# A fused interaction network on one core: first block of x in two half tables, transfers reordered, dummy products in TensorE's waits

## The chip, the cores and the metric

The kernel runs on one core of a Trainium2 chip. The metric is device microseconds of one execution, the median of several runs. Before the change it is 750.26 us (three runs, 749.74 to 750.42). The engines are called PE (TensorE, matrix products), DVE (VectorE), ACT (ScalarE), POOL (GpSimd) and SP (SyncE). ACT, SP and POOL also issue transfers, and all transfers share the core's 16 DMA engines.

## The reference

x has 1024 samples of 39 fields with 64 numbers each. Three layers each multiply the fields of the last layer with those of x in every pair and mix the products by a weight matrix; the sums over the 64 numbers are joined and multiplied by fc_w.

```python
def _cin_layer(Xk, X0, W, b):
    O = W.shape[0]
    Hk, Fdim = (Xk.shape[1], X0.shape[1])
    Wr = W.reshape(O, Hk, Fdim)
    return jnp.einsum('bhe,bfe,ohf->boe', Xk, X0, Wr) + b[None, :, None]
X0 = sparse_embedding
Xk = X0
outs = []
for W, b in ((W0, b0), (W1, b1), (W2, b2)):
    Xk = _cin_layer(Xk, X0, W, b)
    outs.append(Xk.sum(axis=-1))
cin_output = jnp.concatenate(outs, axis=-1)
return cin_output @ fc_w.T + fc_b
```

## The kernel before

Only a weighted sum over the third layer's outputs is needed, so the kernel folds W2 with fc_w into a matrix v2 (v in the profile), and v2 with W1 into a matrix T. W0 and T, transposed, lie in the upper and lower 64 rows of a tile called both. From it DVE and ACT pick the weights (pairs) of each product of two fields; PE transposes them (tr), ACT copies them to wa, and then PE multiplies products of fields (p) by wa and adds them up in po.

x is used in 32 blocks of 32 samples, 2048 columns each. A block of x is first copied within DRAM to a table xd whose rows are fields, with one more row of ones; each table holds two blocks. POOL then gathers rows of the table by lists of indices into r (four tiles for a block), u and v (one pair for two blocks). DVE multiplies two gathered tiles into a p.

```python
    xd = [dram.tile([2 * FT, BLK], F32, name=f"xd{k}") for k in range(NTAB)]

    def load(n, engine=nc.sync):
        first = n % 2 * FT
        engine.dma_start(
            xd[n // 2 % NTAB][first : first + F].rearrange("f (b e) -> f b e", e=E),
            xv[:, n * BB : (n + 1) * BB, :],
        )

    def gather_rows(dst, n, k, cols=slice(0, BLK)):
        table = xd[n // 2 % NTAB][: FT if k < 4 else 2 * FT]
        nc.gpsimd.indirect_dma_start(
            dst[:, cols], None, table,
            bass.IndirectOffsetOnAxis(ap=lists[:, k : k + 1], axis=0),
            element_offset=cols.start,
        )
# ... cut: roll gathers the four r tiles of a block, roll_half gathers u and v
        nc.sync.dma_start(fcrow, fc_w)
        nc.scalar.dma_start(w2s, w2.rearrange("o (s n) -> (o s) n", s=2))
        load(0)
        load_ones(0, nc.scalar)
        for s, n in enumerate((NW, F - NW)):
            nc.scalar.dma_start(w0s[H * s : H * s + F, 0 : n * H], w0v[:, s * NW * H : (s * NW + n) * H])
        for s, engine in enumerate((nc.sync, nc.scalar)):
            engine.dma_start(w1s[H * s : H * s + H], w1[:, s * (FH // 2) : (s + 1) * (FH // 2)])
# ... cut
        nc.scalar.copy(warm, warm)          # ACT loads its table of functions here
        for k in range(1, NTAB):
            load_ones(k, nc.sync)
# ... cut
        def spin(n=1):                      # dummy products, whose result nobody reads
            for _ in range(n):
                nc.tensor.matmul(idle[:, 0 : MM // 2], zeros[:, 0:128], zeros, start=True, stop=True)
# ... cut: the index lists
        halves = [slice(0, SUB), slice(SUB, BLK)]
        for cols in halves:
            roll(0, (0, 1, 2), cols)
        load(1, nc.gpsimd)
        roll(0, (3,))
# ... cut: W2 times fc_w gives pv, then v2; W0 is transposed to pw; lists for u and v
        roll_half(0)
        roll(1)
# ... cut: the biases
        load(2, nc.gpsimd)
        load(3, nc.gpsimd)
        copies = (nc.vector.tensor_copy, nc.scalar.copy)
# ... cut: untwine copies transposed fields from PSUM to both, with the engine given
        for s, (a, n) in enumerate(((0, NW), (NW, F - NW))):
            untwine(copies[s], 0, a, n, 1, pw[s], F)
        # ... v2 times W1: 2 products into pv (fields 32 to 38), 4 into pt (fields 0 to 31)
        # ... pv is copied to rest, pt to part, half by DVE and half by ACT
        turn_fields(pt[0], rest, slice(0, FT), NR)
        untwine(copies[0], 1, 2 * NA, NR, 1, pt[0], FT)
        for k in range(2):
            turn_fields(pw[k], part, slice(H * k, H * k + FT), NA)
        for k in range(2):
            untwine(copies[k], 1, NA * k, NA, NA // 2, pw[k], FT)
        spin(2)
```

Then comes the main part. The products of the first three steps are made in halves, PE starts with the first quarter of the first product, and DVE works four steps ahead of PE. A step is one pair of tiles of one block: six steps with r for each block, and one step with u and v for two blocks, the seventh of the first.

```python
    for k, (n, c) in enumerate(steps[:3]):
        p[n, c] = first[k]
        weight_rows(c)
        if not k:
            weight_turn(c)
            spin()
            for m in range(2):
                product(n, c, slice(m * MM, (m + 1) * MM), p[n, c])
        else:
            product(n, c, halves[0], p[n, c])
# ... cut: second halves, fourth product, and the main loop
```

Of the kernel before, what the change touches and what calls it, by code (L numbers as in the profile page):

```python
# [54 lines left out]
F32 = mybir.dt.float32  # L55
# [5 lines left out]
B, F, E, H = 1024, 39, 64, 64  # L61
FH = F * H
# [13 lines left out]
SUB = 1024  # L76
BLK = 2048
NA = 16
NR = F - 2 * NA
NW = 20  # L80
BB = BLK // E
SB = SUB // E
NBLK = B // BB
FT = F + 1
NTAB = 3
# [13 lines left out]
def cin_kernel(ctx: ExitStack, tc: tile.TileContext, x, w0t, b0, w1, b1, w2, b2, fc_w, fc_b, out):  # L99
    nc = tc.nc  # L100
# [4 lines left out]
    dram = ctx.enter_context(tc.tile_pool(name="dram", bufs=1, space=DRAM))  # L105
# [3 lines left out]

    xv = x.rearrange("b f e -> f b e")  # L110
    xd = [dram.tile([2 * FT, BLK], F32, name=f"xd{k}") for k in range(NTAB)]

    def bank(name):
        return psum.tile([128, MM], F32, name=name, tag="po")
# [5 lines that stand above are left out]
            xv[:, n * BB : (n + 1) * BB, :],  # L120
        )

    def gather_rows(dst, n, k, cols=slice(0, BLK)):
        table = xd[n // 2 % NTAB][: FT if k < 4 else 2 * FT]
        nc.gpsimd.indirect_dma_start(  # L125
            dst[:, cols],
            None,
            table,
            bass.IndirectOffsetOnAxis(ap=lists[:, k : k + 1], axis=0),
            element_offset=cols.start,  # L130
        )

    def roll(n, tiles=range(4), cols=slice(0, BLK)):
        for i in tiles:
            gather_rows(rt[n % 2][:, i], n, n % 2 * 4 + i, cols)

    def roll_half(n):
        gather_rows(ut[n // 2 % 2], n, 8)
        gather_rows(vt[n // 2 % 2], n, 9)

    wa = const.tile([128, NCHUNK, 2 * H], F32, name="wa")
    fc = const.tile([H, 3], F32, name="fc")
# [8 lines left out]
    lists = const.tile([128, 10], I32, name="lists")  # L151
    rt = [const.tile([128, 4, BLK], F32, name=f"r{k}") for k in range(2)]
    ut = [const.tile([128, BLK], F32, name=f"u{k}") for k in range(2)]
    vt = [const.tile([128, BLK], F32, name=f"v{k}") for k in range(2)]
# [17 lines left out]
    with prep as prep:  # L172
        w2s = prep.tile([128, FH // 2], F32, name="w2s")
        w1s = prep.tile([128, FH // 2], F32, name="w1s")
        w0s = prep.tile([128, NW * H], F32, name="w0s")
        part = prep.tile([128, NA, H], F32, name="part")
# [4 lines left out]
        ones = prep.tile([16, 2, 128], F32, name="ones")  # L181
# [7 lines left out]

        nc.vector.memset(zeros, 0.0)  # L193
        nc.vector.memset(ones, 1.0)
        nc.vector.memset(fc2, 0.0)
        nc.vector.memset(v2, 0.0)
        nc.vector.memset(warm, 0.0)

        def load_ones(k, engine):
            engine.dma_start(xd[k][F::FT].rearrange("r (p c) -> p r c", c=128), ones)  # L200

        w0v = w0t.rearrange("b a h -> b (a h)")
        nc.sync.dma_start(fcrow, fc_w)  # L203
        nc.scalar.dma_start(w2s, w2.rearrange("o (s n) -> (o s) n", s=2))
        load(0)
        load_ones(0, nc.scalar)
        for s, n in enumerate((NW, F - NW)):
            nc.scalar.dma_start(w0s[H * s : H * s + F, 0 : n * H], w0v[:, s * NW * H : (s * NW + n) * H])
        for s, engine in enumerate((nc.sync, nc.scalar)):
            engine.dma_start(w1s[H * s : H * s + H], w1[:, s * (FH // 2) : (s + 1) * (FH // 2)])  # L210
        nc.gpsimd.iota(place, pattern=[[0, 1]], base=0, channel_multiplier=1)
        for i in range(3):
            for k, by in enumerate((STEP[i + 1], BASE[i + 1], EXTRA[i + 1] - K)):
# [3 lines left out]
        bothv = both.rearrange("p (a b) -> p a b", b=FT)  # L217
        nc.gpsimd.memset(bothv[0:H, :, F], 0.0)
        nc.scalar.copy(warm, warm)
        for k in range(1, NTAB):  # L220
            load_ones(k, nc.sync)


        pv = [bank("pv") for _ in range(2)]
        pt = [bank("pt") for _ in range(2)]
        idle = bank("idle")
        pw = [bank("pw") for _ in range(2)]
# [3 lines left out]
        def spin(n=1):  # L231
            for _ in range(n):
                nc.tensor.matmul(idle[:, 0 : MM // 2], zeros[:, 0:128], zeros, start=True, stop=True)  # L233
# [45 lines left out]
        for s in range(2):  # L279
            nc.gpsimd.tensor_copy(fcrow2[:, :, s], fcrow[:, 2 * H : 3 * H])  # L280

        halves = [slice(0, SUB), slice(SUB, BLK)]
        for cols in halves:
            roll(0, (0, 1, 2), cols)
        load(1, nc.gpsimd)
        roll(0, (3,))


        one = ones[0:1, 0, 0:1]
# [36 lines left out]
        for s in range(2):  # L326
            for k in range(NW // 2):
                n = min(128, (F - NW * s) * H - k * 128)
# [20 lines left out]
        nc.vector.tensor_scalar(half, half, float(FT), None, ALU.mult)  # L349
        nc.vector.tensor_scalar(lists[:, 8:10], fields_of[:, 4:6], half, None, ALU.add)  # L350
        roll_half(0)
        roll(1)
        for k, t in enumerate((b1, b2)):
            nc.gpsimd.dma_start(bias[:, k : k + 1], t.rearrange("(h o) -> h o", o=1))
# [7 lines left out]
        copies = (nc.vector.tensor_copy, nc.scalar.copy)  # L362

        def untwine(copy, half, a, n, by, src, width):


            for s in range(2):
                m = (n + 1 - s) // 2
                at = a + s * by
                step = 2 if by == 1 else 1  # L370
                copy(  # L371
                    bothv[H * half : H * half + H, at : at + step * (m - 1) + 1 : step, 0:width],
                    src[H * s : H * s + H, 0 : m * FT].rearrange("p (a b) -> p a b", b=FT)[
                        :, :, 0:width
                    ],
                )

        for s, (a, n) in enumerate(((0, NW), (NW, F - NW))):
            untwine(copies[s], 0, a, n, 1, pw[s], F)
        w1v = w1s.rearrange("o (h f) -> o f h", f=F)  # L380
        for s in range(2):
            rows = slice(H * s, H * s + H)
# [23 lines left out]
        def turn_fields(to, src, rows, n):  # L406
            for a in range(0, n, 2):
                m = min(2, n - a)
                nc.tensor.transpose(  # L409
                    to[0 : m * H, a // 2 * FT : a // 2 * FT + FT],  # L410
                    src[rows, a : a + m, :].rearrange("b a h -> b (a h)"),
                    unit[rows, rows],
                )

        turn_fields(pt[0], rest, slice(0, FT), NR)
        untwine(copies[0], 1, 2 * NA, NR, 1, pt[0], FT)
        for k in range(2):
            turn_fields(pw[k], part, slice(H * k, H * k + FT), NA)
        for k in range(2):
            untwine(copies[k], 1, NA * k, NA, NA // 2, pw[k], FT)  # L420
        spin(2)
        first = [prods.tile([128, BLK], F32, name="p", tag="p") for _ in range(3)]


# [128 lines left out]
    p = {}  # L553
# [14 lines left out]
    n, c = steps[3]  # L568
# [98 lines left out]
```

## Time and profile before

| engine | busy us | share of the span |
|---|---|---|
| PE | 740.6 | 99% |
| DVE | 643.9 | 86% |
| POOL | 324.4 | 43% |
| ACT | 163.8 | 22% |

The profiled execution has a span of 750.1 us. PE is busy nearly all of it, so the questions are how long its first products into po must wait, and whether it ever waits afterwards. Busy shares don't show the first; it is read from the chain of work that ended last, in order of time, from the timeline of the first 60 us and from short windows with the clock that PE was granted. In the chain a line gives start, length and what it was. In the timeline a bracket gives the idle time of that engine before the instruction and what ended it. Matmuls are pipelined and their ends are modelled.

The transfers of the start, by the list of DMA issues: w2 624 KB, each half of w1 312 KB, a block of x 312 KB, w0 195.0 and 185.2 KB. In the first 12 us the queue of SP moved 1439 packets with 0.67 MB, that of ACT 376 packets with 1.36 MB: x goes in packets of 256 bytes, since a field of a sample is 64 numbers.

### The profile page before, as it was taken

Reading aid. Unit: us, or ns where it says so; the run is one execution under the profiler, and the core shown is the slowest. Engines: PE = TensorE matmul, PEld = TensorE weight load, DVE = VectorE, ACT = ScalarE, POOL = GpSimd, SP = SyncE. Lnnn points to the kernel's source line nnn. Section 1 sums busy time; section 2 is a strip of 40 time slices with the busy share of each in tenths; the row PEclk is TensorE's granted clock in tenths of the full one; section 3 lists DMA queues with packets and bytes.
Section 4 is the critical chain, followed back from the end, with each engine's and each line's share of the span. In section 5 each row is a group of like instructions: output and inputs, shape, how many; then the busy total and the mean of one; then the engine's idle time right before and its main releaser. Section 6 shows DMA issues by size and latency. Waiting matters only on the chain.

```text
span 750.1 us, 5270 instructions
## 1 busy us (share of the span) xinstructions
PE 740.6 (99%) x1905; PEld 324.1 (43%) x1905; DVE 643.9 (86%) x511; ACT 163.8 (22%) x222; POOL 324.4 (43%) x193
## 2 busy tenths in 40 slices
PE   7999999999999999999999999999999999999998
PEld 4444444444444444444444444444444444444443
DVE  5989899888899888899888898888899888898885
ACT  2132112221212222112221212222112221212222
POOL 4679952436243263532436343263532436343100
PEclk8899999999999999999999999999999999999999
DMA  6899885865757776575865757776576854737400
GB/s 175 301 320 378 320 343 198 336 245 198 286 168 291 258 268 251 184 288 197 336 246 202 280 169 292 259 273 241 194 266 215 335 224 175 289 142 291 168 1 0
DMA packets 58791, 180.07 MB, mean 240 GB/s; under 512 B 37079, under 2 KB 37176, under 8 KB 38669
## 3 DMA queue, kind: packets, MB, share of 16 engines
q0 software_dynamic: 24160, 169.39, 59.2%
q1 hardware_dynamic: 34227, 8.98, 5.3%
q10 hardware_dynamic: 378, 1.37, 0.7%
q8 instruction: 15, 0.25, 0.1%
q14 instruction: 11, 0.09, 0.0%
HBM read 179.66 MB, written 10.28 MB: 253 GB/s over the span
## 4 chain that ended last, share of the span: by engine, by line
PE 97%; DMA 1%; DVE 0%; issue 0%; ACT 0%; SPq 0%; ACTq 0%
PE po L485 96%; DMA w1s<-in_w 1%; PE idle L233 0%; PE pt L389 0%; PE tr L469 0%; SPq L118 0%; PE pv L383 0%; ACT both L371 0%; PE pw L409 0%; DVE g L524 0%; DVE sums L526 0%; ACT zq L523 0%; DVE pairs L434 0%; PE pt L409 0%; SPq L203 0%
## 5 line engine op out<-in xcount | busy, mean ns | idle before, releaser
L485 PE MATMUL po<-p,wa 128*128 128x512 f32 (+1 forms) x1792 | 723.2, 595 | 0.0
L166 DVE TENSOR_TENSOR p<-r 128x2048 f32<-128x2048 f32 (+2 forms) x196 | 434.9, 2247 | 86.3 <-PE po L485 83.6
L485 PEld LDWEIGHTS po<-p,wa 128*128 128x128 f32 (+1 forms) x1792 | 314.0, 190 | 405.5 <-issue 384.1
L125 POOL DMA_INDIRECT r<-xd,lists x131 | 265.2, 2025 | 357.1 <-DVE p L166 325.2
L504 ACT ACTIVATE z<-po,fc0s 64x512 f32<-64x512 f32 x124 | 84.9, 685 | 356.3 <-PE po L485 349.5
L498 ACT COPY g<-u 39x1024 f32<-39x1024 f32 x64 | 66.7, 1043 | 181.8 <-DVE sums L515 181.7
L510 DVE SCALAR_TENSOR_TENSOR g<-po,b0s,z 64x512 f32<-64x512 f32 x124 | 86.4, 734 | 0.0
L515 DVE TENSOR_REDUCE sums<-g 103x16 f32<-103x1024 f32 x62 | 75.6, 1220 | 2.2
L125 POOL DMA_INDIRECT u<-xd,lists x16 | 32.3, 2022 | 10.5 <-DMA xd<-in_x 5.9
L168 DVE TENSOR_TENSOR p<-u,v 128x2048 f32<-128x2048 f32 x16 | 36.6, 2285 | 0.0
L125 POOL DMA_INDIRECT v<-xd,lists x16 | 17.2, 1074 | 4.9 <-issue 4.9
L233 PE MATMUL idle<-zeros 128*128 128x256 f32 x14 | 6.3, 591 | 1.2 <-DVE zeros L193 1.2
L524 DVE SCALAR_TENSOR_TENSOR g<-po,b0s,zq 64x512 f32<-64x512 f32 x4 | 3.0, 743 | 5.3 <-ACT zq L523 5.3
L434 DVE TENSOR_TENSOR pairs<-both 128x6 f32<-128x6 f32 (+27 forms) x50 | 5.4, 179 | 1.7 <-ACT both L371 1.7
L470 ACT COPY wa<-tr 128x128 f32<-128x128 f32 x7 | 1.9, 266 | 19.8 <-PE tr L469 19.8
L118 POOL DMA_DIRECT2D xd<-in_x x5 | 5.2, 1044 | 0.0
L523 ACT ACTIVATE zq<-po,fc0s 64x512 f32<-64x512 f32 x4 | 2.7, 684 | 10.2 <-PE po L485 10.2
L469 PE MATMUL tr<-unit,pairs 128*128 128x128 f32 x7 | 2.2, 319 | 2.4 <-DVE pairs L434 2.4
L233 PEld LDWEIGHTS idle<-zeros 128*128 128x128 f32 x14 | 3.6, 289 | 1.7 <-DVE zeros L193 1.2
L335 DVE STREAM_TRANSPOSE blocks<-pv 128x320 f32<-128x320 f32 x2 | 1.0, 518 | 2.7 <-PE pv L314 2.7
L383 PE MATMUL pv<-w1s,v 64*64 64x224 f32 x4 | 1.1, 602 | 2.1 <-DMA w1s<-in_w 2.1
L469 PEld LDWEIGHTS tr<-unit,pairs 128*128 128x128 f32 x7 | 1.1, 159 | 4.5 <-ACT both L371 2.7
(90 smaller groups left out, 45.6 us busy)
## 6 DMA issues: line engine op xcount, KB each, us to landing
xd<-in_x SPq DMA_DIRECT2D x27, 312.0 KB
r<-xd,lists POOLq DMA_INDIRECT x131, 7.8
xd<-in_x POOLq DMA_DIRECT2D x5, 312.0 KB, 5.7
w2s<-in_w ACTq DMA_DIRECT2D x1, 624.0 KB
w1s<-in_w SPq DMA_DIRECT2D x1, 312.0 KB
w1s<-in_w ACTq DMA_DIRECT2D x1, 312.0 KB
u<-xd,lists POOLq DMA_INDIRECT x16
v<-xd,lists POOLq DMA_INDIRECT x16, 9.0
```

The costliest lines, as they stand in the source:

```text
L118: engine.dma_start(xd[n // 2 % NTAB][first : first + F].rearrange("f (b e) -> f b e", e=E), xv[:, n * BB : (n + 1) * BB, :],)
L125: nc.gpsimd.indirect_dma_start(dst[:, cols], None, table, bass.IndirectOffsetOnAxis(ap=lists[:, k : k + 1], axis=0), element_offset=cols.s ...
L166: nc.vector.tensor_tensor(p[:, cols], r[:, i, cols], r[:, k, cols], ALU.mult)
L168: nc.vector.tensor_tensor(p, ut[n // 2 % 2], vt[n // 2 % 2], ALU.mult)
L233: nc.tensor.matmul(idle[:, 0 : MM // 2], zeros[:, 0:128], zeros, start=True, stop=True)
L434: nc.vector.tensor_tensor(out, diagonal(a, b, sa, sb), diagonal(b, a, sb, sa), ALU.add)
L469: nc.tensor.transpose(tr[:, at], pairs[:, c], unit)
L485: nc.tensor.matmul(po[n + h][m], wa[w, c, :], p[w, bass.ts(m, MM)], start=c == opens[n + h], stop=c == closes[n + h],)
L498: nc.scalar.copy(gt[H : H + F], ut[n // 2 % 2][h : h + F, bass.ts(m, SUB)])
L504: nc.scalar.activation(z[m // 2][:, bass.ts(m % 2, MM)], po[n][m][H:128], AF.Identity, bias=fc0s[H:128])
L510: nc.vector.scalar_tensor_tensor(gt[0:H, at], po[n][m][0:H], b0s, z[m // 2][:, at], ALU.add, ALU.mult)
L515: nc.vector.tensor_reduce(sums[:, b_at : b_at + SB], gt.rearrange("p (b e) -> p b e", e=E), AX.X, ALU.add)
```

## The change

The aim is an earlier start of the main part. The first block of x is copied into two half tables of 1024 columns each, xh, so that the first gathers need only half of it. ACT's queue takes w2, w0, the first half of x, half of w1 and the second half of x; SP's queue takes the other half of w1 and no x. The full table's copy of the first block, which u, v and block 1's gathers use too, is loaded by POOL after the gathers from the half tables; the rows of ones come from POOL and SP. Of the transposes of T, the upper pw goes first, then the lower pw, then pt, and ACT rather than DVE empties pt. Dummy products are put after the transposes of W0 and after the products of W1, and two become three after the transposes of T; they are meant to keep PE's clock from falling.

```diff
+    xh = [dram.tile([FT, SUB], F32, name=f"xh{k}") for k in range(2)]
@@
         nc.scalar.dma_start(w2s, w2.rearrange("o (s n) -> (o s) n", s=2))
-        load(0)
-        load_ones(0, nc.scalar)
         for s, n in enumerate((NW, F - NW)):
             nc.scalar.dma_start(w0s[H * s : H * s + F, 0 : n * H], w0v[:, s * NW * H : (s * NW + n) * H])
-        for s, engine in enumerate((nc.sync, nc.scalar)):
-            engine.dma_start(w1s[H * s : H * s + H], w1[:, s * (FH // 2) : (s + 1) * (FH // 2)])
+        for k in range(2):
+            nc.sync.dma_start(xh[k][F:FT].rearrange("r (p c) -> p r c", c=128), ones[0:8, 0:1])
+        nc.sync.dma_start(w1s[0:H], w1[:, 0 : FH // 2])
+        for k in range(2):
+            nc.scalar.dma_start(
+                xh[k][0:F].rearrange("f (b e) -> b f e", e=E), x[k * SB : (k + 1) * SB]
+            )
+            if not k:
+                nc.scalar.dma_start(w1s[H:128], w1[:, FH // 2 : FH])
@@
-        for k in range(1, NTAB):
-            load_ones(k, nc.sync)
@@
+        for k in range(NTAB):
+            nc.gpsimd.dma_start(xd[k][F::FT].rearrange("r (p c) -> p r c", c=128), ones)
+
         halves = [slice(0, SUB), slice(SUB, BLK)]
-        for cols in halves:
-            roll(0, (0, 1, 2), cols)
+        for k, cols in enumerate(halves):
+            for i in range(3):
+                gather_rows(rt[0][:, i, cols], xh[k], i)
         load(1, nc.gpsimd)
-        roll(0, (3,))
+        for k, cols in enumerate(halves):
+            gather_rows(rt[0][:, 3, cols], xh[k], 3)
+        load(0, nc.gpsimd)
@@
             untwine(copies[s], 0, a, n, 1, pw[s], F)
+        spin()
@@
-        turn_fields(pt[0], rest, slice(0, FT), NR)
-        untwine(copies[0], 1, 2 * NA, NR, 1, pt[0], FT)
-        for k in range(2):
-            turn_fields(pw[k], part, slice(H * k, H * k + FT), NA)
-        for k in range(2):
+        spin()
+        for k in (1, 0):
+            turn_fields(pw[k], part, slice(H * k, H * k + FT), NA)
+        turn_fields(pt[0], rest, slice(0, FT), NR)
+        for k in (1, 0):
             untwine(copies[k], 1, NA * k, NA, NA // 2, pw[k], FT)
-        spin(2)
+        untwine(copies[1], 1, 2 * NA, NR, 1, pt[0], FT)
+        spin(3)
```

Gathers now take the table itself as an argument; that part of the diff, and the line of the half tables' size, move no work and are cut.

More of the change, by code (lines that the diff above doesn't have):

```diff
@@ L121, in load, with gather_rows, roll @@
         )
-    def gather_rows(dst, n, k, cols=slice(0, BLK)):
-        table = xd[n // 2 % NTAB][: FT if k < 4 else 2 * FT]
+    def gather_rows(dst, table, k):
         nc.gpsimd.indirect_dma_start(
[L126 to L130, printed above, removed]
-        )
-    def roll(n, tiles=range(4), cols=slice(0, BLK)):
-        for i in tiles:
-            gather_rows(rt[n % 2][:, i], n, n % 2 * 4 + i, cols)
+            dst, None, table, bass.IndirectOffsetOnAxis(ap=lists[:, k : k + 1], axis=0)
+        )
+    def roll(n):
+        for i in range(4):
+            k = n % 2 * 4 + i
+            gather_rows(rt[n % 2][:, i], xd[n // 2 % NTAB][: FT if k < 4 else 2 * FT], k)
     def roll_half(n):
-        gather_rows(ut[n // 2 % 2], n, 8)
-        gather_rows(vt[n // 2 % 2], n, 9)
+        for k, dst in enumerate((ut, vt)):
+            gather_rows(dst[n // 2 % 2], xd[n // 2 % NTAB], 8 + k)
     wa = const.tile([128, NCHUNK, 2 * H], F32, name="wa")
@@ L197, in cin_kernel @@
         nc.vector.memset(warm, 0.0)
-        def load_ones(k, engine):
-            engine.dma_start(xd[k][F::FT].rearrange("r (p c) -> p r c", c=128), ones)
         w0v = w0t.rearrange("b a h -> b (a h)")
```

## The prediction

> **What bounds the kernel now.** I read the page first: TensorE (PE) is busy 99% of the span, so only its first stretch can hold anything. Then the chain that ended last, in order of time, cut to the first 60 us (start us, us, what):
>
> ```profile
> 2.15 9.83 DMA w1s<-in_w
> ...
> 12.12 0.74 PE pv L383 x2
> ...
> 15.93 0.38 PE pt L409 x4
> 16.31 0.78 PE pw L409 x16
> 17.09 1.65 PE idle L233 x4
> ...
> 18.76 0.43 ACT both L371
> ...
> 20.52 0.45 PE tr L469
> 20.97 0.85 PE idle L233 x2
> 21.82 1.71 PE po L485 x2
> ...
> 23.74 2.33 PE po L485 x4
> ...
> 26.18 6.87 PE po L485 x16
> ```
>
> From 21.82 us on the chain is the products into po and nothing else. 16 entries take 6.87 us, so one 512-column product (two entries) takes 0.859 us. 768 full products make 659.7 us. The 46 entries that the chain puts between 42.08 and 58.79 us (16.71 us) hold 15 full products (12.9 us) and the four side-by-side pairs of a half step, so a pair takes 0.956 us and the 64 pairs 61.2 us. With 21.82 us before them, 1.46 us lost at the start (below), six tr of 0.11 us and 0.33 us of pk, the last product ends at 745.2 us; the timeline has 745.1. So the middle has no slack to win. The time is the start of the first po, plus what PE loses after it, plus a tail of 5 us that the change leaves alone.
>
> Next the timeline of the first 60 us, for what stands close behind that chain (start, us, engine, line, operation, then idle time before and its releaser):
>
> ```profile
> 11.77 1.17 POOL L125 DMA_INDIRECT r<-xd,lists  x1 [8.67 <-DVE both L371]
> 20.29 1.29 DVE L166 TENSOR_TENSOR p<-r 128x512 f32<-128x512 f32 x2
> 28.49 1.35 POOL L125 DMA_INDIRECT u<-xd,lists  x1 [5.91 <-DMA xd<-in_x]
> 30.18 2.29 DVE L166 TENSOR_TENSOR p<-r 128x2048 f32<-128x2048 f32 x1 [0.77 <-DMA r<-xd,lists]
> 42.98 2.29 DVE L166 TENSOR_TENSOR p<-r 128x2048 f32<-128x2048 f32 x1 [1.57 <-DMA r<-xd,lists]
> ```
>
> GpSimd (POOL) can gather only once the whole first block of x is in its table. The release named, DVE, was no condition of this instruction beyond the list that DVE had ready by 3.9 us; the program makes it wait for the x transfer, so I read 11.77 as x landing. The gathers land 6.8 us after issue by the view of the table, the second (issued 13.24) at about 20.0, and the first product, which needs both, starts at 20.29. So the gathers are nearly as late as the weights: both must move.
>
> Last the windows of one microsecond (PE, PEld, DVE, ACT, POOL, granted clock, DMA share, GB/s):
>
> ```profile
> 10.00:11.00 1.00, 0.00 (x0) 0.00 (x0) 0.93 (x5) 0.93 (x2) 0.00 (x0) 1.00 0.27 80
> 12.00:13.00 1.00, 0.88 (x7) 0.82 (x11) 0.00 (x0) 0.00 (x0) 0.94 (x1) 0.50 0.00 0
> 17.00:18.00 1.00, 1.00 (x6) 0.68 (x4) 0.96 (x2) 0.00 (x0) 0.92 (x1) 1.00 0.84 160
> 22.00:23.00 1.00, 1.00 (x2) 0.23 (x1) 1.00 (x3) 0.00 (x0) 0.58 (x1) 0.50 1.07 430
> 25.00:26.00 1.00, 1.00 (x4) 0.42 (x3) 1.00 (x2) 0.00 (x0) 0.00 (x0) 1.00 0.96 356
> ```
>
> The clock is at half when T is made and again for the first three products: 1.71 + 2.33 us in place of 3 x 0.859, the 1.46 us above.
>
> [...] finer windows put the changes at about 11.2, 14.6, 18.03 and 24.85 us, which are 3.4, 3.4 and 6.8 apart. [...] In the trace the first half of W1 stands behind x in SyncE's queue and lands at 11.98, with x, although 1.95 MB in all had moved by about 10.3. [...] here 1 to 1.7 us lie between the last bytes and the landing.
>
> **The change, part by part.**
>
> Transfers. Bytes before the first gather fall. Before, w2 (639 KB), w0 (389), x (319) and most of w1 (639) had to pass. After, ScalarE's queue (ACT) has w2, w0, half of x (160), half of w1, half of x; SyncE's has only the other half of w1 (320). Ahead of half x stand 639 + 389 + 320 + 160 = 1508 KB. The DMA rates of 0 to 12 us in 40 slices sum to 1454 KB at 7.2 us, so 1508 KB pass at about 7.5. The half table goes in 624 small packets without much to run beside, so I add 0.5 us, then 1.5 to 2 us of landing in DRAM: 9.5 to 10.0. That is about 2 us before 11.77. The second half of w1 follows by 0.9 us of data and lands near 9.9, again 2 us earlier. One catch: its issue now waits until w2 has landed (they share a semaphore). SyncE's wait for w2 ended at 4.72 before, so that is in time. The activation table load on ACT slides from 3.6 to about 6.5, still before ACT's first need at 8.8.
>
> T. PE's transposes of W0 end at 9.97, then one dummy (0.43). The w1 products start at about 10.5 and not 12.12. They took 3.0 us, mostly at half clock; at full clock I estimate 1.8. DVE and ACT still end their W0 copies at 11.66 and 10.95, no longer hidden, so I take part of it back: T's copies at 12.7 to 13.4, not 15.1.
>
> Upper transposes first. Before, DVE emptied pt (0.62) and pw (0.99), ACT one pw (0.86), but ACT began only at 18.76 although its transposes are modelled to end at 17.09. After, ACT does the upper pw and then pt (1.48), DVE one pw (0.99); both begin while PE still transposes. If ACT starts promptly, transposes to last copy take about 2.2 us in place of 3.7. So weights would be ready 2.0 (transfers) + up to 1.2 (clock) + 1.5 (copies) = 3 to 4.7 us earlier. The gathers, 2 us earlier, now end last: the first product moves from 20.29 to about 18.2.
>
> Dummies. Three more come in waits, 0.43 us each at full clock, and nothing waits for them beyond PE's own order. If they hold the clock, the first three products gain 1.46 us. But DVE was only 0.6 us ahead of PE at the fourth product (ended 32.47, PE began at 33.16), plus the 0.77 us that it waited for r. So at most 1.3 us of it counts, and only if r comes earlier too.
>
> What gives back. u, v and block 1 need the full table, whose first block now loads last on POOL. Gathers from 9.7, six at 1.25 us, a load, two half gathers and the load: it is issued near 21, where before the load of block 1 was issued at 19.17. Ahead of it stand 4.2 MB of gathers and 0.3 MB of x from 10.5 us on; at the 296 GB/s that the same stretch averaged before (4.5 MB from 13.0 to 28.2) with 0.32 MB more they end at about 26.8, and land at 28 to 29. So u still starts at about 28.5, and block 1's first product stays near 42.98 to 45.27. PE wanted it at 48.2: 2.9 us of slack. u times v ends at 41.4 and was wanted at 44.6: 3.2 us. These cap the gain at 3 us, give or take one.
>
> Sum: about 2.0 us from the gathers, up to 1.3 from the clock, 30% likely to be kept in full, capped at 3: some 2.3 us. 750.26 - 2.3 = 747.9.
>
> **The rivals.** First, u and the table behind it come later than 28.5 (small packets amid gathers are slow: u came free 9.3 us after the load of block 1 was issued at 19.17): each microsecond over 29.5 comes off one for one; it could leave 749 to 751. Second, transfers don't gain: half x in small packets on ACT's queue delays w1, or w2 is slowed by w1 beside it (both large packets, where x was small), and v2 moves the whole chain: 749.5. Third, everything fits: weights at 17, clock held, table at 27: 746. Against the third speaks the 0.6 us of DVE's lead; against the second, that PE had v2 only at 9.6 and w2 at 4.72, with a microsecond to spare.
>
> **Range and chances.** All parts lie in a start of 22 us out of 750; two percent would be 15 us, more than the start can yield or a wait for one table can cost. Range 746.2 to 749.8: from the cap plus one to a gain almost all given back.
>
> **What would show it.** First half-table gather at 9.5 to 10; first w1 product near 10.5; first po at 19 to 19.7; ACT's copy of the upper transposes right behind its transposes; clock 1.0 at the first po if the dummies work; u's gather at 28 to 29; PE waiting about 44 to 47 us only if the cap binds. It is wrong if PE idles there over 1 us, or if the gathers begin no earlier than 11.

## The result, and the profile after

| | median us | range | n |
|---|---|---|---|
| before, in this comparison | 750.34 | 749.74 to 751.21 | 4 |
| changed | 751.12 | 750.11 to 752.90 | 4 |

The ratio of changed to before is 1.0012, 95% interval 0.9989 to 1.0035. Two later comparisons with the same kernel gave 1.0019 (1.0003 to 1.0034) and 1.0040 (1.0028 to 1.0053). By these medians the change costs one to four parts in a thousand, though the first interval still holds 1. The prediction said 747.9 (746.2 to 749.8); the time moved the other way.

The profiled execution of the changed kernel has a span of 748.3 us (its time was 750.11, at the low end), where that of before had 750.1 (its time was 751.83, above the four in the table). PE is again busy 99% (740.9 us). One line of the list of costliest groups is new in kind: the products into po have idle time ahead of them, and it is one wait.

```profile
L489 PE MATMUL po<-p,wa 128*128 128x512 f32 (+1 forms) x1792 | 722.5, 595 | 2.6 <-DVE p L163 2.6
```

The chain that ended last, in order of time (start us, us, what), shows where that wait comes from. Before, it was the products into po from 21.82 us on. Now po does not come into it until 46.31:

```profile
...
19.58 1.29 POOL r L125
...
20.88 6.44 DMA xd<-in_x
...
28.15 1.29 POOL u L125
29.44 0.31 issue
29.75 2.80 POOL v L125
32.55 0.30 issue
32.85 2.72 POOL r L125
35.58 0.30 issue
35.88 8.00 DMA r<-xd,lists
...
43.96 2.30 DVE p L163
46.26 0.04 issue
46.31 10.57 PE po L489 x24
```

Read it from the end. Block 1's first product p waits for a gather r; that gather stood behind u and v on POOL; u waited for the last load of the full table; that load was issued at 20.88, after all half-table gathers. W1, T and the weights, which the change makes earlier, are not in the chain at all. They don't set the time any more.

The timeline (start, us, engine, line, operation, idle time before and releaser) at the places that were shown of before:

```profile
9.39 1.06 POOL L125 DMA_INDIRECT r<-xh,lists  x1 [4.54 <-DVE v L344]
14.88 0.86 ACT L373 COPY both<-pw 64x320 f32<-64x320 f32 x2 [0.89 <-PE pw L412]
17.87 1.13 PE L489 MATMUL po<-p,wa 128*128 128x512 f32 x2
28.15 1.29 POOL L125 DMA_INDIRECT u<-xd,lists  x1 [6.23 <-DMA xd<-in_x]
43.96 2.29 DVE L163 TENSOR_TENSOR p<-r 128x2048 f32<-128x2048 f32 x1 [4.17 <-DMA r<-xd,lists]
46.31 10.57 PE L489 MATMUL po<-p,wa 128*128 128x512 f32 x24 [2.57 <-DVE p L163]
```

The start did all that was hoped: gathers from 9.39 (before 11.77), first product into po at 17.87 (before 21.62 in the timeline), with the granted clock at full from 8 us to near the end. Then PE arrives at block 1 at 43.74 and stands still for 2.57 us. The windows (length; busy PE, PEld, DVE, ACT, POOL; clock; DMA share; GB/s) have the hole, and 16 us earlier another one, in the DMA engines:

```profile
26.00:28.00 2.00, 2.00 (x6) 0.86 (x5) 1.83 (x3) 0.00 (x0) 0.00 (x0) 1.00 0.03 10
28.00:30.00 2.00, 2.00 (x7) 0.86 (x6) 2.00 (x12) 0.53 (x3) 1.54 (x2) 1.00 0.00 0
...
44.00:45.00 1.00, 0.00 (x0) 0.00 (x0) 1.00 (x1) 0.45 (x1) 0.83 (x1) 1.00 1.01 385
```

From 26 to 30 us the DMA engines move next to nothing, as POOL waits for the table and then issues slowly; at 44 PE is idle while they are busy all the time (share 1.01).

### The profile page after: what moved, and what is told of

It reads as the page before. It is cut to its first block, busy times and chain, and to the rows that moved or that the text cites. A ratio compares the mean times of both kernels' runs of the same rounds, so it can differ in the third digit from the quotient of the medians.

```text
span 748.3 us, 5288 instructions
## 1 busy us (share of the span) xinstructions
PE 740.9 (99%) x1911; PEld 322.9 (43%) x1911; DVE 643.1 (86%) x509; ACT 164.2 (22%) x224; POOL 319.6 (43%) x198
## 4 chain that ended last, share of the span: by engine, by line
PE 94%; POOL 2%; DMA 2%; DVE 1%; issue 1%; ACT 0%; POOLq 0%; DVEq 0%
PE po L489 93%; POOL r L125 1%; DMA r<-xd,lists 1%; DMA xd<-in_x 1%; PE idle L229 1%; POOL v L125 0%; PE pv L316 0%; DVE p L163 0%; POOL u L125 0%; POOL xd L119 0%; DVE g L528 0%; DVE sums L530 0%; ACT zq L527 0%; DVE blocks L337 0%; PE small L296 0%
## 5 line engine op out<-in xcount | busy, mean ns | idle before, releaser
L125 POOL DMA_INDIRECT r<-xd,lists x124 | 247.6, 1996 | 352.9 <-DVE p L163 331.8
L125 POOL DMA_INDIRECT r<-xh,lists x8 | 8.3, 1034 | 6.7 <-DVE v L344 4.5
L373 DVE COPY both<-pw 64x390 f32<-64x390 f32 (+1 forms) x4 | 2.1, 523 | 1.1 <-PE pw L412 1.1
L392 PE MATMUL pt<-w1s,v 64*64 64x512 f32 x8 | 2.9, 1124 | 0.0
```

The source lines that it names most:

```text
L125: nc.gpsimd.indirect_dma_start(dst, None, table, bass.IndirectOffsetOnAxis(ap=lists[:, k : k + 1], axis=0))
```

## The experiments

Every ratio is to the kernel before, run beside it on the same chip. Labels with "after" start from the changed kernel, those with "before" from the other. T1 below: the time is set by block 1's first product, so an earlier start is given back; the least time that this leaves is called the floor. Rivals: the start itself isn't earlier on average; the dummies; the order of the transposes.

### Both kernels once more

No edit.

> The changed kernel once more, to see whether its runs differ by more than those of before and where. Theory (late table): first po near 17.9 us and clock 1.0 as in its first profile, but TensorE waits about 2.6 us at block 1's first product for the gathers behind the table that loads last; time within 0.3% of before, since the 4 us won at the start are given back there, more in executions in which the table lands later. Rival (clock): the start is what varies; in a longer execution the clock is at half at the first po and there is little wait at block 1.

> The kernel before once more, ratio 1.00. Its one profile (span 750.1) was of one of its longer executions. Theory (late table): no wait of TensorE between 25 and 60 us in this one either, and a first po between 20 and 22 us. Rival (clock): in a shorter execution the first po is at full clock, which alone makes 1.3 us.

after_again: 752.43 us, ratio 1.0019 (1.0003 to 1.0034). before_again: 751.57, ratio 1.0004 (0.9994 to 1.0014). The profiles were a surprise. The changed kernel, timeline:

```profile
14.99 0.86 ACT L373 COPY both<-pw 64x320 f32<-64x320 f32 x2 [1.20 <-PE pw L412]
17.84 0.99 DVE L373 COPY both<-pw 64x320 f32<-64x320 f32 x2 [4.01 <-PE idle L229]
18.58 0.55 ACT L373 COPY both<-pt 64x160 f32<-64x160 f32 x2 [2.73 <-remote]
21.13 1.92 PE L489 MATMUL po<-p,wa 128*128 128x512 f32 x2
```

and the kernel before:

```profile
9.66 1.17 POOL L125 DMA_INDIRECT r<-xd,lists  x1 [6.56 <-DVE tmp L251]
18.27 0.86 ACT L371 COPY both<-pw 64x320 f32<-64x320 f32 x2 [3.58 <-remote]
25.73 3.62 POOL L125 DMA_INDIRECT u<-xd,lists  x1 [6.31 <-DMA xd<-in_x]
44.91 2.29 DVE L166 TENSOR_TENSOR p<-r 128x2048 f32<-128x2048 f32 x1 [3.92 <-DMA r<-xd,lists]
47.26 10.57 PE L485 MATMUL po<-p,wa 128*128 128x512 f32 x24 [0.24 <-DVE p L166]
```

Three readings. First, in before the gathers began at 9.66 here and at 11.77 in the first profile: what I took for the property of the order of transfers is no larger than the spread of one execution to the next. Second, the late copy of T's upper part, 18.76 us in before, also strikes the changed kernel, with its other order: both copies that follow ACT's first start 2.5 to 3 us late, the clock is at half from about 18.9 to 25.7, and po starts at 21.13, where before starts. Third, before waits 0.24 us at block 1 as well: in this execution it stands right at the same limit.

### The floor: earlier, later, elsewhere

load0_early issues the missing load two half gathers earlier; load0_twice issues it a second time, to delay u without touching anything before it:

```diff
 # load0_early
+        load(0, nc.gpsimd)
         load(1, nc.gpsimd)
         for k, cols in enumerate(halves):
             gather_rows(rt[0][:, 3, cols], xh[k], 3)
-        load(0, nc.gpsimd)
 # load0_twice
         load(0, nc.gpsimd)
+        load(0, nc.gpsimd)
```

> The changed kernel with block 0's full table loaded ahead of block 1's, so both loads are issued before the two half gathers of the fourth tile. Theory (late table): the u gather starts at 25 to 26 us and not 28.2, block 1's first two r tiles land 2 to 3 us earlier, TensorE's wait at block 1 (2.6 us) falls under 0.6, and the time is 2 to 2.6 us under the changed kernel's. Rival (bandwidth): the transfers' total is the limit, the r tiles of block 1 land at 43.9 all the same and the time stays; or the fourth tile of block 0, now behind the loads, makes TensorE wait near 26 us instead.

> The changed kernel with block 0's full-table load issued twice at the end of the same place, so that u waits for one more load. Theory (late table): u starts 1.5 to 3 us later than 28.2, TensorE's wait at block 1 grows by the same, and so does the time, one for one. Rival (bandwidth or something else holds block 1): under 0.7 us, what 0.32 MB more cost.

load0_twice: 756.99 us, ratio 1.0079 (1.0064 to 1.0094). u came at 34.00 and the wait at u times v was 6.50 us:

```profile
34.00 3.23 POOL L125 DMA_INDIRECT u<-xd,lists  x1 [4.17 <-DVE p L163]
38.82 0.94 POOL L125 DMA_INDIRECT r<-xd,lists  x1 [0.30 <-issue]
45.53 2.29 DVE L165 TENSOR_TENSOR p<-u,v 128x2048 f32<-128x2048 f32 x1 [8.66 <-DMA v<-xd,lists]
50.50 2.29 DVE L163 TENSOR_TENSOR p<-r 128x2048 f32<-128x2048 f32 x1 [2.68 <-DMA r<-xd,lists]
```

5.85 us later at u, 6.5 us later at block 1's product (50.50 for 43.96), 7.1 us more of span (755.4 for 748.3). Of these, 1.3 are a later start (po from 19.21) and 3.9 a longer wait (6.50 for 2.57). The rest, some 1.9, fits the clock: from 45.0 to 51.8, in the wait and after it, PE had half of it, and of the 3.83 us of this that it was busy half counts as lost: the weight loads of po come in pairs every 0.86 us up to 51.52 and every 0.43 us from 52.10. The same followed the wait at block 1 in after_no_tail (half from 49.8 to 53.3) and in after_no_spins (50.6 to 54.0), but not in the first profile of the changed kernel. So once the start is early, a late table is paid for, in part through the clock. The medians differ by less, 4.6 us (752.43 to 756.99); after_again's profiled execution had a late copy in place of the wait.

load0_early: 751.58 us, ratio 1.0004 (0.9992 to 1.0016). Its profiled execution again had the late copy (po from 21.77), so PE didn't wait at block 1. Its four executions with a clock of 0.999 or 1.0 had spans of 747.1, 747.5, 748.5 and 748.5, where after_again's two at 1.0 had 748.4 and 749.5: an earlier table may help a little. The gathers can be read, and they show one reason why it helped no more in the profiled execution:

```profile
24.33 4.62 DVE L163 TENSOR_TENSOR p<-r 128x1024 f32<-128x1024 f32 x4
26.57 3.33 POOL L125 DMA_INDIRECT u<-xd,lists  x1 [3.82 <-DMA xd<-in_x]
30.21 2.43 POOL L125 DMA_INDIRECT v<-xd,lists  x1 [0.30 <-issue]
43.76 2.29 DVE L163 TENSOR_TENSOR p<-r 128x2048 f32<-128x2048 f32 x1 [3.00 <-DMA r<-xd,lists]
```

and the windows of the same execution:

```profile
28.00:30.00 2.00, 2.00 (x7) 0.80 (x6) 2.00 (x8) 0.00 (x0) 1.90 (x1) 1.00 0.00 0
```

u was released 1.58 us earlier than in the first profile, block 1's product moved 0.20. The issue of u took 3.33 us, and it ended 0.95 us after the products that run from 24.33 to 28.95; from 28 us until then no byte moved. An issue takes 0.94 when DVE is idle, as in load0_twice. In before_again the u gather ended 1.06 us after DVE's product and the next three 0.82 to 0.96 after theirs. So it looks as if a gather that is issued while DVE multiplies two gathered tiles does its 0.94 us of work only when the product is over. Over all 20 profiles, in the first 57 us, 122 of the 123 gathers begun in a product with at least 0.2 us of it left took 1.15 to 5.28 us and ended 0.81 to 1.11 us after it, or after the unbroken row of products that it was in. The exception is one in late_again (17.39 us, 0.94 with 0.72 us of product left). A plain load of x that POOL issues inside a product is not held up, where a gather in loads_sp_late took 5.18 us for 0.94. In the changed kernel's first profile, 0.20 us into the product that starts at 43.96:

```profile
44.16 0.94 POOL L119 DMA_DIRECT2D xd<-in_x  x1 [0.29 <-DMA r<-xd,lists]
```

All 37 plain loads of x begun with over 1.15 us of a product left took 0.94 to 1.12 us. What sets the gathers and these loads apart is not shown.

The rival of load0_early, that the transfers' total is the limit, is not excluded. r landed at 43.8 all the same, and the DMA engines were busy 0.66 to 1.03 of the time in the windows of 2 us from 30 to 44. From the end of u's issue to block 1's product 13.9 us pass here, 14.5 in the first profile and 13.3 in load0_twice. That stretch is much the same in all three; what these edits move is when it begins.

The next takes both loads off POOL and puts them on SyncE's queue, held back by a small copy that needs the first part of W0:

```diff
 # loads_sp
+    held = dram.tile([1, H], F32, name="held")
@@
+        nc.sync.dma_start(held, w0s[0:1, 0:H])
+        load(0)
+        load(1)
@@
-        load(1, nc.gpsimd)
@@
-        load(0, nc.gpsimd)
```

> The changed kernel, with both loads of the first full table issued by SP as soon as w0 has landed (a 256-byte copy holds them back), instead of by POOL among its gathers. Theory (the gathers of u, v and block 1 are made while DVE multiplies, and each then lasts until DVE's product ends: 2.3 to 3.6 us in place of 0.94): u is issued at about 19 to 20 us and not 28, block 1's second r tile by 27 and not 35.9, TensorE's wait at block 1 goes to zero whatever the start was, and time is 1 to 2.5 us under before (748.5 to 750). Rival (transfer rate is the limit): r lands at 42 or later all the same and the time stays at 751 to 752. Second rival: the two loads beside W1 and the half tables delay the first gather by 1 to 2 us and eat the gain.

749.0 us (748.42 to 749.89, n = 14), ratio 0.9994 (0.9985 to 1.0002). u was issued at 23.49 (19 to 20 was expected), and PE waits nowhere at block 1; the last figure of its group, idle time before the products into po, is 0.0:

```profile
23.49 2.86 POOL L126 DMA_INDIRECT u<-xd,lists  x1 [0.30 <-DVE pairs L440]
L491 PE MATMUL po<-p,wa 128*128 128x512 f32 (+1 forms) x1792 | 722.2, 595 | 0.0
```

The floor is gone. The loads cost the front what they gave the back: first gather 11.57, W1 products 12.54, po 20.17, and that, with nothing lost later, is 748.1 us of span (749.89 us, the longest of its 14; the shortest had 746.6). A place of the loads that doesn't disturb W1 was the obvious next step: hold them for the upper half of W1 instead.

```diff
 # loads_sp_late, and the same a second time as late_again
-        nc.sync.dma_start(held, w0s[0:1, 0:H])
+        nc.sync.dma_start(held, w1s[H : H + 1, 0:H])   # after the half gathers
```

> The changed kernel with the two loads of the first full table on SyncE's queue, held until the upper half of W1 has landed, and no longer in the way of the half tables. Theory (time is set by block 1's first product, which waits for gathers of a table that is loaded last and are issued in VectorE's products): first gather 9.3 to 11, W1 products 10.2 to 11.5, gather of u issued at 22 to 25, no TensorE wait at block 1 above 0.3 us; where the copies of T aren't late, first product near 18 and the span near 747; ratio 0.997 to 0.999. Rival (the loads must end somewhere, and now take the DMA engines from the first block's own gathers): first product waits for r at 18 to 21, ratio 1.000 to 1.002.

> Control, the kernel loads_sp_late unchanged. In its first profile TensorE's signals for the last 8 upper transposes (ending at instruction 186 of TensorE's stream, where a product in float32 counts as four: two weight loads and two passes) and for the 4 rest transposes came at 19 and 21.2 us instead of 15.7 and 15.9, and all its runs were near 754.7. Both theories: again a late copy of T, 753 to 757.

Twice the same kernel, on two chips, two answers: 754.69 us, ratio 1.0051 (1.0033 to 1.0068), and 749.91 us, ratio 1.0011 (0.9996 to 1.0025). In neither profile does PE wait at block 1, as T1 said. What differs in the profiles is the late copy of T. The first:

```profile
15.50 0.86 ACT L375 COPY both<-pw 64x320 f32<-64x320 f32 x2 [1.48 <-PE pt L414]
19.04 0.99 DVE L375 COPY both<-pw 64x320 f32<-64x320 f32 x2 [4.98 <-issue]
21.19 0.55 ACT L375 COPY both<-pt 64x160 f32<-64x160 f32 x2 [4.83 <-remote]
23.73 1.91 PE L491 MATMUL po<-p,wa 128*128 128x512 f32 x2
```

and the second, whose span of 746.8 us is 1.5 under the first profile of the changed kernel:

```profile
15.02 0.99 DVE L375 COPY both<-pw 64x320 f32<-64x320 f32 x2 [1.12 <-PE pw L414]
18.76 1.02 PE L491 MATMUL po<-p,wa 128*128 128x512 f32 x2
```

My expectation of late_again, which took the late copy for a property of this kernel, was wrong.

The same idea in the kernel before, without and with the added dummies (its load of block 1 behind W1 on SyncE's queue):

```diff
 # before_load1_sp (and, with the three dummies of the change, before_load1_sp_spins)
-        load(1, nc.gpsimd)
         roll(0, (3,))
+        nc.sync.dma_start(held, w1s[H : H + 1, 0:H])
+        load(1)
```

> The kernel before with only its second load of the table moved from GpSimd's to SyncE's queue, behind the upper half of W1. Theory: u is issued at 22 to 25 instead of 25.7 to 28.5, block 1's product no longer waits, but TensorE, which starts its products at 20 to 21.6, did not wait for it before either: ratio 0.9985 to 1.0005. Rival (the floor is already felt in the kernel before): ratio 0.997 to 0.9985.

> The same with the added dummy products as well. Theory: with the floor gone, the held clock (up to 1.4 us) is kept instead of given back: ratio 0.9975 to 0.999, first product near 19.6 with the clock at 1.0. Rival (it is the late copies of T and not the clock that vary): same as without the dummies, 0.9995 to 1.0005.

754.0 us, ratio 1.0043 (1.0020 to 1.0066), and 756.3 us, ratio 1.0043 (1.0011 to 1.0075); the 756.3 is the median of nine executions from 748.4 to 760.9, and the ratio leaves out two, of 760.5 and 760.9, that lie over 1.5% above the fastest. The tables came even earlier than expected (u at 20.26 and 19.91), PE didn't wait at block 1, and yet both lost: ACT's copy of T started at 19.91 and 18.95 and po at 23.81 and 23.63. Both expectations missed.

### The dummies and the rest

```diff
 # before_spins: the kernel before with the added dummies alone
         untwine(copies[s], 0, a, n, 1, pw[s], F)
+        spin()
@@
+        spin()
         turn_fields(pt[0], rest, slice(0, FT), NR)
@@
-        spin(2)
+        spin(3)
 # after_no_tail, loads_sp_no_tail
-        spin(3)
 # after_no_spins
-        spin()
@@
-        spin()
@@
-        spin(3)
+        spin(2)
```

> The kernel before with only the dummy products of the change: one after the transposes of W0, one after the products of W1, three at the end. If the clock were the point, the first po finds full clock more often and the time falls by up to 1.3 us. If block 1's gathers are the floor, as in the second profile of before (TensorE waited 0.24 us there), it falls by under 0.5 us.

> The changed kernel without the three dummy products after T's transposes. In four of six profiles DVE or ACT started to copy T's transposes 2.5 to 3 us after they were modelled to end, with dummies queued behind them. Theory A (dummies delay it): no such wait, first po near 17.9 in every profile, but the clock may be at half there; time up to 1 us under the changed kernel. Theory B (something else delays it): the wait comes as often as before, the time is that of the changed kernel or 0.5 us over it, since the clock drops.

> Both edits: loads of the first table from SP, and no dummies after T's transposes. With theory A it is the fastest of all, 747 to 748.5; with theory B it is within 0.7 us of the run with SP's loads alone.

> The changed kernel without its three added dummy products. Theory of the floor: the clock falls to a half somewhere in T, first product 19 to 21, block 1's product stays at 43.5 to 46, ratio 1.000 to 1.003, no worse than with the dummies. Rival (the dummies are what the change lives on): 1.004 or more.

before_spins: 749.88 us, ratio 1.0004 (0.9992 to 1.0016). The clock was at 1.00 from 9 us to the first po at 19.61, as was hoped of the dummies, and no copy was late (ACT 16.41). But PE then ran ahead of the gathers, and waited 1.4 us in three pieces for DVE's products; nothing was won.

after_no_tail: 750.99 us, ratio 1.0023 (1.0014 to 1.0033), po from 18.63, the clock at half from 19.1 to 22.5, and still 2.60 us of waiting at block 1 (its profiled execution, 753.76, is one of the longest of 20). loads_sp_no_tail: 750.18 us, ratio 1.0009 (1.0001 to 1.0017): beside loads_sp in the same comparison, the tail is worth about 1.2 us where there is no floor, though only the two medians say so; neither of the two forecasts for it came true. after_no_spins: 752.2 us, ratio 1.0010 (1.0002 to 1.0019), late copies (DVE 17.37, ACT 18.82), po from 21.35, u at 29.26 and 2.06 us of waiting at block 1.

### Moving the start

To see whether the late copies go with a place in TensorE's stream of instructions, early dummies were cut into shorter ones, which moves everything behind them back by 16, 48 or 36 instructions (a product counts as four: in the trace the two dummies at 1.2 us are four weight loads and four matmuls).

```diff
 # late_shift16: six of 85 columns for the first two of 256; late_shift48 and after_shift48: twice eight of 64
-        spin(2)
+        short(6)
 # after_tiny: one of two dummies becomes ten of 1 row, 64 weights, 1 column
-        spin(2)
+        spin()
+        tiny(10)
```

> The same with the first two dummy products cut into six shorter ones of the same total width: all later instructions of TensorE stand 16 places further back in its stream. Theory of the place (TensorE runs out of instructions at a place of its stream between 171 and 186, whatever stands there): the stall comes one group earlier, at the transposes that ScalarE copies first, so that ScalarE's first copy of T starts after 17 us as well, not at 15.5. Rival (it is those transposes, or their operands, that are late): ScalarE's first copy at 15.5, VectorE's at 18 to 19 as before.

> The same with the first four dummy products as sixteen shorter ones: 48 places further back. Theory of the place: the copies of T follow their transposes directly (ScalarE at 15.5, VectorE at 15.8); a stall, if there is one, stands at the W1 products at 10.4 to 13.5[...]; with first product at 18 to 19 and no wait at block 1 the time is 746.5 to 749, ratio 0.994 to 0.998. Rival: late copies as in the control, 753 to 757.

> The changed kernel with the same sixteen shorter dummies. Theory of the place: no late copy in any execution, so all runs are like the good ones of the changed kernel, first product at 17.9 to 19 with the clock at 1.0, but the wait at block 1 (u's table) stays: 748.5 to 751, ratio 0.998 to 1.000, with the clock of every run at 0.998 or more. Rival: as the changed kernel, 1.001 to 1.003 and clocks down to 0.995.

> Control for the next: the changed kernel unchanged, a third time. 750 to 752.5, ratio 1.001 to 1.003, with some executions at a mean clock of 0.995 (those with a late copy of T), as 3 of 9 were the last time.

> The changed kernel with one of the four early dummy products replaced by ten tiny ones (1 row, 64 weights, 1 column; about 0.1 us each), which moves all later instructions of TensorE 36 places back in its stream at hardly any time. Theory of the place: no execution at a clock under 0.998, the copies of T directly behind their transposes, spans within 1 us of 748.5 and the median 0.5 to 1 us under the control's. Rival (the late copies have to do with the time or the transposes, not with the place): the same share of executions at 0.995 as the control, and the same median within 0.3 us.

On the question asked they decide nothing: neither the four shifted ones nor the two unshifted ones beside them (late_again, after_third) had a late copy. But the shifts cost time, which I had not expected (late_shift48 was to come to 746.5 to 749), and so became the cleanest test of T1. After the sixteen short dummies, po starts 3.25 us later than in after_third, after the tiny ones 1.42 later. The unmoved kernel, after_third (752.03 us, ratio 1.0040, 1.0028 to 1.0053), timeline:

```profile
17.88 1.12 PE L489 MATMUL po<-p,wa 128*128 128x512 f32 x2
44.95 2.29 DVE L163 TENSOR_TENSOR p<-r 128x2048 f32<-128x2048 f32 x1 [4.25 <-DMA r<-xd,lists]
47.30 10.57 PE L489 MATMUL po<-p,wa 128*128 128x512 f32 x24 [2.74 <-DVE p L163]
```

and after_shift48 (750.9 us, ratio 1.0027, 1.0017 to 1.0038):

```profile
21.13 1.12 PE L494 MATMUL po<-p,wa 128*128 128x512 f32 x2
40.60 16.87 PE L494 MATMUL po<-p,wa 128*128 128x512 f32 x46
43.64 2.29 DVE L163 TENSOR_TENSOR p<-r 128x2048 f32<-128x2048 f32 x1 [3.06 <-DMA r<-xd,lists]
```

3.25 us of start taken away, and the span is 748.7 for 749.3: not longer, shorter. after_tiny (751.02 us, ratio 1.0033, 1.0017 to 1.0048) starts at 19.30 and has 749.7. late_shift16 came to 749.7 us, ratio 1.0016 (0.9998 to 1.0033), late_shift48 to 750.85, ratio 1.0021 (1.0014 to 1.0029). In late_shift48 u was issued only at 28.75, though its loads left at 10.9 and 11.9 us (late_again: 19.88): loads on SyncE's queue are not always early.

In executions with the full clock from the first po on, one sum fits: the span is the first po, plus what PE waits after it, plus a constant.

| kernel | first po | waits after | sum | span | span less sum |
|---|---|---|---|---|---|
| changed | 17.87 | 2.57 | 20.44 | 748.3 | 727.9 |
| after_third | 17.88 | 3.19 | 21.07 | 749.3 | 728.2 |
| after_tiny | 19.30 | 2.52 | 21.82 | 749.7 | 727.9 |
| after_shift48 | 21.13 | 0 | 21.13 | 748.7 | 727.6 |
| loads_sp | 20.17 | 0 | 20.17 | 748.1 | 727.9 |
| late_shift16 | 19.19 | 0 | 19.19 | 747.2 | 728.0 |
| late_again | 18.76 | 0.41 | 19.17 | 746.8 | 727.6 |

(Waits under 0.15 us are left out. The 3.19 of after_third are 2.74 at block 1, 0.27 at u times v and 0.18 earlier. late_shift48, with 21.10, no wait and 749.0, fits with 727.9, and so does before_spins, with 19.61, 0.77 and 748.3.) With the table loaded last, the sum stays at 20.4 to 21.8 (the first four rows), whether po starts at 17.9 or at 21.1. Without that (the last three rows) it is the start that counts.

## Why the prediction was wrong

Its steps one by one.

**Transfers.** First gather 9.5 to 10 and W1 products near 10.5 were predicted; 9.39 and 10.39 came (the 1.5 to 2 us of landing in the sum were an estimate, from the 1 to 1.7 read in before), and 9.30 to 11.26 and 10.19 to 11.49 in other profiles with the changed order of transfers and its dummies. Right as places. Wrong as a gain: "2 us before 11.77" measured the change against one execution of before. before_again has 9.66 and 10.78.

**T and the clock.** Predicted: first po at 19 to 19.7, clock held. The first profile did better, 17.87 at full clock. after_again, with the late copy, had 21.13 at half. That dummies hold the clock was an assumption: with the same ones it stayed at 1.00 in before_spins and fell to half at 18.9 in after_again. What moves it is not shown here: in before, PE was busy for 2.67 of the 3.43 us from 14.6 to 18.0, 1.16 of them with transposes, and the clock went to 0.50; the changed kernel has the same 1.16 us of transposes, from 14.18 on, and kept 1.00. The products of W1, put at 1.8 us with the full clock, took 2.91 at 1.00 (10.39 to 13.30).

**Upper transposes first.** Here a step fell. I read ACT's start at 18.76 us, behind transposes that were modelled to end at 17.09, as a cost of the order, and took 1.5 us for it. It is no matter of the order: before_spins has the old order and ACT at 16.41, and after_again has the new one and DVE at 17.84.

**The cap.** Predicted: u at 28 to 29, block 1's product staying at 42.98 to 45.27, PE there in need of it at 48.2 before, so a gain of at most about 3. u came at 28.15. PE came to block 1 4.5 us earlier (43.74) and the product ended 1.0 us later (46.25), so 2.57 were waited for and 1.9 kept: 750.1 to 748.3 of span. Between these two profiles the working was nearly right, 1.8 us for 2.3. But the term "block 1's first product stays near 42.98 to 45.27" was mis-sized: the product ended at 46.25, at 47.24 in after_third and at 48.36 in after_no_tail. u wasn't late. The gathers behind it were, most of them held up by DVE's products (v 2.80 us, the first r 2.72, the last 2.25); I had counted only the table's landing, and of the first rival only "u later than 28.5".

**The sum.** "750.26 - 2.3 = 747.9" is the step that failed. The 2.3 us came out of a profile of an execution that took 751.83 us, 1.6 over the median of before; they were then taken off the median, in which most of that loss isn't contained. Taken off the profile's own span they give 747.8, where 748.3 came. And with block 1's product where it is, the changed kernel has a floor there: none of its 19 timed executions in three comparisons had a span under 748.3 us, which is 750.1 of time. Before reached as little as 748.1 beside 748.4 of the changed kernel in the comparison of after_again, and 746.1 beside 749.3 in that of after_third. Before's median of 750.34 is a span of about 748.5, so the median had next to no room to fall. Why it rose can be read only from single profiles: block 1's gathers ended a microsecond or two later (after_third), a copy was late (after_again), or the clock fell to half after the wait at block 1 (after_no_tail). Which share each has is not shown.

**What was won.** Clock, but not time. In the comparison of after_third, the mean granted clock is 0.997 to 1.0 in all six executions of the changed kernel, with spans of 749.3 to 751.0. It is 0.995 or less in nine of the 14 of before; the other five, at 0.997 and 0.998, have 746.1 to 747.4. Whether the start was won is less clear. Both profiles of before, with a first po at 21.62 and 21.12, had a late copy and half the clock. By the sum above, an estimate for before, its fastest execution beside late_again (span 745.1) leaves 17.2 us for the first po and all that is lost after it, less than the first po of any profile, and its median there (747.7) leaves 19.8. With the floor gone, the medians are 749.91 for late_again beside 749.49 of before, and 749.0 for loads_sp beside 749.65. So the loss at block 1 is shown, but no median shows a start earlier than that of before's usual execution.

The sign that I had written for "wrong" was met: PE idles over 1 us at 44 to 47.

## What stays open

Whether the start is earlier on average, the first rival above: no profile of before without a late copy is at hand to compare with.

The late copies themselves. In 8 of 20 profiles copies of T start 1.7 to 3.7 us (one, of pt in loads_sp_late, 5.8) after the transposes are modelled to have ended. The trace's semaphore events put it on PE's side: in after_again PE signals ACT's eight transposes at 14.97, DVE's at 17.82, the rest at 18.56 and the three dummies behind them at 19.33, though all are recorded as started by 16.4. In the profiles without it the signals follow at once (14.86, 15.14, 15.36, 16.85 in the changed kernel). It strikes both kernels, with and without dummies. All four kernels of one comparison had it, none of six in the next two. It isn't the chip alone: chip 8 had it in three of four profiles in one comparison and in none of four in a later one. In none of the eight is a transfer of instructions in the trace between the start and the late copy, so that PE ran out of instructions is not supported; nor is crowding of the DMA engines, which were as busy in loads_sp (share 1.08 to 1.15 at 12 to 16 us) without it. I have no cause.

No version beat both kernels. loads_sp comes nearest, 0.9994 of before with an interval that holds 1. late_again shows 746.8 us of span in one execution, but not as a median, and before has single executions under that.

## What to carry to other kernels

A start that is made earlier pays only up to the first later wait that hangs on other data. Follow that data's own chain (the last load, the queue of issues behind it, what each issue contends with) before you count the gain, and remember that moving a load to the end to free the start sets that wait. Profile the kernel before more than once: a gain that is read from an execution slower than the median must be taken off that execution, not off the median. And an indirect gather by GpSimd is best issued while VectorE isn't multiplying gathered tiles: here it took 0.94 us then, and up to 5.28 otherwise.

## What I had not expected of the hardware

The issue of an indirect gather on GpSimd takes 0.94 us beside an idle VectorE, and 1.15 to 5.28 us when it begins in one of VectorE's products, ending 0.81 to 1.11 us after that product or the unbroken row it is in (122 of 123). A gather that begins just ahead of products can be caught too: in load0_twice that of u began at 34.00, among VectorE's small products and 0.05 us before a large one, and took 3.23. Plain loads of x issued by GpSimd are not held up (37 of 37, 0.94 to 1.12 us). In load0_early the DMA engines moved nothing for 2 us, from 28 to 30, with a gather waiting.

Dummy products of few columns aren't free: sixteen of 64 columns in place of four of 256 moved TensorE's next product, W2's, from 5.71 to 8.91 us, and ten of one column in place of one of 256 moved it to 7.07.

The start of one and the same kernel differs by up to 2 us between executions already at its first gathers (before: 9.66, 11.51 with dummies, 11.77).
